# Layer 1 of a two-layer attention kernel: a block's values copied out in front of its softmax sums, one k addition moved behind two z additions, and the first two score copies exchanged between two engines

## The chip, the cores and the metric

The kernel runs on one core of one Trainium2 chip, as one program of about 131,000 instructions. The metric is the device time of one execution in microseconds, taken as the median of several runs. A profiled execution was recorded beside them. Its trace gives every instruction's start and duration on each engine: TensorE (PE for its matmuls, PEld for its weight loads), VectorE (DVE), ScalarE (ACT), GpSimd (POOL) and SyncE (SP, whose queue starts most of the transfers).

## The reference, cut to what matters

The input is x with 8 batch elements of 512 channels and 32 x 32 positions, in fp32. Layer 0 is a group norm, an attention of 8 heads and a projection, with a residual. The change touches layer 1 alone. For each batch element b, T = 1024 positions, 8 heads g of 64 channels:

```python
q, k, v = w_q @ xf, w_k @ xf, w_v @ xf           # xf = group_norm(x), per head 64 x 1024
attn = einsum('bhdq,bhdT->bhqT', q, k) * scale   # scores
attn = einsum('gh,bhqT->bgqT', w_head, attn)     # heads mixed
attn = softmax(attn, axis=-1)
attn = (attn - mean) / sqrt(var + EPS)           # over all (q, T) of a head
attn = attn * in_gamma + in_beta
out  = einsum('bhqT,bhdT->bhqd', attn, v)        # values
out  = out.reshape(b, t, c) @ w_proj.T + b_proj
x    = x + out
```

The kernel uses that the row sums of a softmax are 1, so that only the sum of squares has to be collected for the variance. It multiplies the exponentials with v first, and divides by the row sums later.

## The kernel before, in words

**Tiling.** Layer 1 takes the batch elements one after the other. The 1024 queries of an element are cut into NQB = 4 blocks of 256, the keys into 4 blocks of 256. One pair of blocks is done in two half-steps, so an element has NX = 32 of them, and a query block has QLAG = 8. The work is software-pipelined in `half_step(x)`, called with x = 0 to 36. It issues the scores of half-step x, the head mixing of half-step y = x - 4 (MLAG is 4) and the sums and values of half-step w = x - 5. No scheduler moves anything: each engine executes its instructions in the order in which the code issues them, and waits on semaphores for its operands and buffers.

**What a half-step issues.**
- `scores(x, i)` for i = 0, 1: 16 matmuls (L1656) into one PSUM tile of tag m, of which there are three buffers. It is then copied to SBUF into `raw`, on DVE (L1671) or on ACT (L1673). When both copies of an odd half-step are issued, eight transfers on SP's queue regroup `raw` into `re` (L1682), so that heads lie along partitions. Each is issued behind a particular matmul.
- `mix(y, j)` for j = 0, 1: 64 matmuls (L1706) with the head weights into another m tile, and ACT's exp from there to `e` (L1712).
- `squares(w, j)` on ACT (L1723), `sum_e` on DVE (a copy, L1728, in the first half-step of a block, then additions, L1730) and `sum_e2` on DVE (L1734). They collect the sums z and the sums of squares z2 over the eight half-steps of a block. In the first half-step of a block the squares are written into z2 directly.
- `values(w, i)` for i = 0, 1: 8 matmuls (L1752) into the accumulators a0 and a1, one PSUM bank each and with one buffer each. They run over the eight half-steps of a block, so the first values of the next block need both emptied.

TensorE's order within a half-step is: scores 0, mix 0, values 0, scores 1, mix 1, values 1.

**The end of a block.** `totals(qb)` is called when the last values of the block are issued. Its 16 matmuls with ones (L1783) sum z2 and then z over the partitions into an m tile. DVE copies one half of that into `row` (L1791), then ACT the other (L1792). Two transfers take `row` into the small tiles c0 and c1 (L1796), on POOL's queue for the blocks 0 to 2 and on SP's for the last. `leave(qb)` empties the accumulators into the attention output, which uses the q buffer: four copies of a1 on DVE (L1772) and four of a0 on ACT (L1774). For the inner blocks it is issued in the next half-step, behind its `scores(x, 0)`, and so behind the row copies. For the last block it is issued behind the whole loop, again behind the row copies. `reciprocals` (L1808, with a transfer to `zd`, L1810, and four broadcasts to `rzb`, L1814) and `divide` (L1842) follow, for the inner blocks 2 and 6 half-steps later.

**The end of an element.** During the last half-steps the k projection of the next element runs in pieces: seven products by TensorE (L1400), whose results DVE adds into sums and into k (L1415 to L1421, L1456). `k_leave()` issues the additions that are due, in each half-step between `sum_e` and `sum_e2`. The last of them, of product 3, is issued in half-step 36. Behind the loop come the last block's totals' consumers, part of the v projection (pv, L1475), a small matmul (pi, L1857) that gives the variance, the division, the affine pass (L1875, L1877), additions on DVE for the projection (L1375), and the output and q projections (pp and pq, L1400). The last element has no next one, and ends with `out1_last`, which interleaves the projection's products with these steps, and loads x again (xs_last, L1577).

**The start of an element.** The scores of half-step 0 need q, whose last parts DVE adds (L1512).

Of the kernel before, what the change touches and what calls it, by code (L numbers as in the profile page):

```python
# [467 lines left out]
def tile_two_attention_layers(  # L468
# [102 lines left out]
    NQB = 4  # L571
# [125 lines left out]
    with ExitStack() as l0:  # L697
# [486 lines left out]
        first = Agenda()  # L1184
# [80 lines left out]
    with ExitStack() as l1:  # L1265
# [14 lines left out]
        NX = 2 * NQB * NKB  # L1280
        QLAG = NX // NQB
        R_ORDER = (0, 4, 1, 5, 2, 6, 3, 7)
        MLAG = 4

        def m_psum(nm):
            return ps_m.tile([P, 2, FB], F32, tag="m", name=nm)
# [29 lines left out]
        def left_piece(key, i):  # L1316

            if i == 0:
                left_tile(key)
            f, r = i // 2, i % 2 * D  # L1320
            return nc.sync.dma_start(
                out=w_t[key][r : r + D, f],
                in_=left_d[key[0] + "1"][r : r + D, f * 2 * HC : (f + 1) * 2 * HC],
            )
# [26 lines left out]
        def y_piece(b, i):  # L1351

            if i == 0:
                y_t[b] = shared.tile([P, NCC, T], F32, tag="n", name=f"y_{b}")
            c, r = i // 4, i % 4 * 32
            return nc.sync.dma_start(
                out=y_t[b][r : r + 32, c], in_=x1_d[b][c * P + r : c * P + r + 32, :]
            )

        def normalize1(b, c):  # L1360
            normalize_to(y_t[b][:, c], b, c)
# [100 lines left out]
        def k_leave():  # L1462
            for fn in due:
                fn()
            due.clear()

        def v_pair(b, i):

            if i == 0:
                v_t[b] = shared.tile([P, NT, C], F32, tag="v", name=f"v1_{b}")  # L1470
            ps = m_psum(f"pv1_{b}_{i}")
            w = w_t["v", b]
            for m in range(2):
                for c in range(NCC):
                    nc.tensor.matmul(  # L1475
                        ps[:, m], y_t[b][:, c, ts(2 * i + m, P)], w[:, c],
                        start=(c == 0), stop=(c == NCC - 1),
                    )
            nc.scalar.copy(v_t[b][:, 2 * i], ps[:, 0])  # L1479
            nc.vector.tensor_copy(v_t[b][:, 2 * i + 1], ps[:, 1])  # L1480
# [158 lines left out]
        class Attention1:  # L1639
# [5 lines left out]
            def scores(self, x, i):  # L1645

                b, t, hp = self.b, x // 2, x % 2 * 2 + i
                qb, kb = t // NKB, t % NKB
                nm = f"s1_{b}_{x}_{i}"
                ps = m_psum(nm)  # L1650
                pv = ps.rearrange("p m (j k) -> p m j k", j=2)
                for j in range(2):
                    for c in range(2):
                        for m in range(2):
                            r = slice(m * D, m * D + D)
                            last = nc.tensor.matmul(  # L1656
                                pv[c * D : c * D + D, m, j],
                                qo_t[b][r, 2 * qb + j, hp, ts(c, D)],
                                k_t[b][r, hp, ts(kb, KB)], start=True, stop=True,
                            )  # L1660
                if x > MLAG:
                    self.piece(last)
                if x % 2 and i == 1:

                    order = (4, 5, 6, 7, 0, 1, 2, 3) if t == 1 else R_ORDER
                    self.due = [(t, r) for r in order]
                if x % 2 == 0 and i == 0:
                    self.raw[t] = rawpool.tile([P, H, 2, KB], F32, tag="raw", name=f"raw_{b}_{t}")
                dst = self.raw[t][:, 2 * hp : 2 * hp + 2]
                if i == 0 and (x < MLAG or x % 2):  # L1670
                    nc.vector.tensor_copy(dst, pv)  # L1671
                else:
                    nc.scalar.copy(dst, pv)  # L1673
# [204 lines left out]

            def half_step(self, x, ag):
                y, w = x - MLAG, x - MLAG - 1  # L1880
                first = 0 < w < NX and w % QLAG == 0
                if first:

                    self.scores(x, 0)
                    self.leave(w // QLAG - 1)
                if 0 <= w < NX:
                    self.squares(w, 0)
                    self.sum_e(w, 0)
                if x < NX and not first:
                    self.scores(x, 0)  # L1890
                if 0 <= w < NX:
                    self.squares(w, 1)
                    self.sum_e(w, 1)
                k_leave()
                if 0 <= w < NX:
                    self.sum_e2(w, 0)
                    self.sum_e2(w, 1)
                if 0 <= y < NX:
                    self.mix(y, 0)
                if 0 <= w < NX:  # L1900
                    self.values(w, 0)
                if x < NX:
                    self.scores(x, 1)
                if 0 <= y < NX:
                    self.mix(y, 1)
                ag.run(x - 0.75)
                if x <= MLAG or x >= NX:
                    self.regroup(n=NR)
                if x >= NX:
                    self.piece(n=len(self.pieces))  # L1910
                ag.run(x - 0.5)
                if 0 <= w < NX:
                    self.values(w, 1)
                    self.e.pop(w)
                    if w % QLAG == QLAG - 1:
                        qb = w // QLAG
                        self.totals(qb)
                        if qb < NQB - 1:
                            ag.at(x + 2, lambda: self.reciprocals(qb, ag, x + 2))
                            ag.at(x + 6, lambda: self.divide(qb))  # L1920
                ag.run(x)
# [5 lines left out]
        for b in range(B):  # L1927
            more = b + 1 < B
            a = Attention1(b)
            ag = Agenda()  # L1930

            for i, slot in enumerate((1, 3 - 0.75)):
                ag.at(slot, lambda i=i: v_pair(b, NV + i))
            if b == 0:
                for x, fn in enumerate(group_stages(B - 1, B, small_psum1)):
                    ag.at(x, fn)
                ag.at(3 - 0.75, v_sums)
            free = (NX // 2 - 2 + b) % 2
            if more:
                a.pieces += [lambda i=i: y_piece(b + 1, i) for i in range(4 * NCC)]  # L1940
                a.pieces += [lambda i=i: left_piece(("k", b + 1), i) for i in range(14)]
                for c in range(NCC):
                    ag.at(24 + c, lambda c=c: normalize1(b + 1, c))

                def k_begin():
                    kp.append(k_projection(b + 1))
                    kp[0].products(1)
                    kp[0].leave(1)

                def k_go(*ms):  # L1950
                    for m in ms:
                        kp[0].products(m)
                        due.append(lambda m=m: kp[0].leave(m))

                kp = []
                ag.at(NX - 0.5, lambda: right_tile(b + 1))
                ag.at(NX - 0.5, k_begin)
                ag.at(NX, lambda: right_y(b + 1, [0, 1]))
                ag.at(NX, lambda: k_go(2))
                ag.at(NX + 1, lambda: right_y(b + 1, [2, 3]))  # L1960
                ag.at(NX + 1, lambda: k_go(6, 7))
                ag.at(NX + 1, lambda: load_w(("v", b + 1), wvT, re_t[:, free, : NCC * C]))
                ag.at(NX + 1, lambda: left_p(b))
                ag.at(NX + 2, lambda: k_go(5, 4))
                ag.at(NX + 3, lambda: k_go(3))
            else:
                a.pieces += [lambda i=i: p_piece(i) for i in range(2 * NCC)]
            for x in range(NX + MLAG + 1):
                a.half_step(x, ag)

            a.leave(NQB - 1)
            if not more:
                ag.flush()
                out1_last(a)
                continue
            a.reciprocals(NQB - 1)
            a.instance()
            ag.flush()
            v_pair(b + 1, 0)
            a.instance_end()  # L1980
            a.divide(NQB - 1)
            for g in range(H):
                a.affine(g)
            right_o = re_t[:, 1 - free].rearrange("p (i k t) -> p i k t", i=4, k=2)
            combine_right(right_o, out_view(b))
            op = out1(b, right_o)
            load_left(("q", b + 1))
            v_pair(b + 1, 1)
            op.run()
            q_projection(b + 1).run()  # L1990
# [70 lines left out]
```

## Time and profile before

| | |
|---|---|
| time, median of 3 runs | 4268.98 us (4268.31 to 4270.03) |
| the profiled execution | 4269.45 us, of which its span 4267.5 us |
| layer 1 | from about 1812 us to the end |
| TensorE clock granted | 0.997 |
| one half-step of layer 1 in its steady part, two groups of scores, mix and values | about 5.94 us |
| VectorE, copy of a 128 x 1024 score tile from PSUM (L1671) | 1223 ns |
| ScalarE, the same (L1673) | 1015 ns |
| VectorE, one copy of 64 x 256 out of an accumulator (L1772) | median 422 ns, 128 of them |
| ScalarE, the same (L1774) | median 367 ns, 128 of them |
| VectorE, row copy (L1791), and ScalarE's (L1792) | 691 and 585 ns, 32 each |
| VectorE, addition of a 128 x 1024 tile (L1730, L1734) | 1218 and 1219 ns |

How to read it: the table's durations are those of single instructions. The lines that show what waits for what stand in the prediction. There, a line of the chain or of the timeline begins with its start and its duration in us, counted from the start of the span; a line of the waits has the total, how often it occurred, and the longest. An engine's name with the letter q means its queue or sequencer.

### The profile page before, as it was taken

What the parts mean: (1) busy time and instruction counts of PE and PEld (TensorE: products, weight loads), DVE (VectorE), ACT (ScalarE), POOL (GpSimd) and SP (SyncE); (2) the same over time, 40 slices, a digit from 0 to 9 for tenths busy, and PEclk for the clock granted to TensorE, in tenths of its full rate; (3) what the DMA queues carried; (4) which work ended last, traced back from release to release, by engine and by line L of the source; (5) the groups of instructions that cost most, each with busy time, mean ns of one, the idle gap of its engine ahead of it and who ended that gap; (6) DMA issues with size and microseconds to landing.
All of it is one profiled execution on the core that took longest, in us unless ns stands there. A gap on an engine that the chain in (4) does not pass through costs nothing.

```text
span 4267.5 us, 131379 instructions
## 1 busy us (share of the span) xinstructions
PE 4158.3 (97%) x58572; PEld 2213.3 (52%) x58572; DVE 2862.8 (67%) x3780; ACT 2319.2 (54%) x2735; POOL 53.3 (1%) x86
## 2 busy tenths in 40 slices
PE   7999999999999999999999999999999999999998
PEld 4353535353535353466466466466466466465565
DVE  4748484848484848558668668578578578587587
ACT  1717171727272726268268278187187286286385
POOL 0000000000000000000000000000000000000000
PEclk9999999999999999999999999999999999999999
DMA  4213131212121212167377287277386385485474
GB/s 148 78 49 109 47 110 45 86 45 85 45 85 45 84 47 83 56 169 192 111 180 190 93 199 186 99 197 185 96 202 166 103 205 155 121 204 142 136 179 136
DMA packets 253872, 521.99 MB, mean 122 GB/s; under 512 B 51889, under 2 KB 59441, under 8 KB 246641
## 3 DMA queue, kind: packets, MB, share of 16 engines
q1 hardware_dynamic: 248416, 510.71, 42.4%
q8 instruction: 461, 7.55, 0.7%
q0 software_dynamic: 2576, 0.69, 0.3%
q10 hardware_dynamic: 2304, 2.10, 0.2%
q14 instruction: 115, 0.93, 0.1%
HBM read 197.16 MB, written 46.92 MB: 57 GB/s over the span
## 4 chain that ended last, share of the span: by engine, by line
PE 90%; DVE 4%; ACT 2%; DMA 2%; issue 1%; SPq 0%; POOL 0%; DVEq 0%; ACTq 0%; POOLq 0%
PE a L1752 11%; PE s L1656 11%; PE m L1706 11%; PE s L1083 10%; PE a L1109 10%; PE pp_p L903 5%; PE pk_p L903 5%; PE pq_p L903 4%; PE pv_p L903 4%; PE pk L1400 4%; PE pq L1400 4%; PE pv L1475 4%; PE pp L1400 3%; PE t L1783 2%; ACT q L1774 1%
## 5 line engine op out<-in xcount | busy, mean ns | idle before, releaser
L1706 PEld LDWEIGHTS m<-wmix,re 64*64 64x64 f32 x32768 | 580.8, 135 | 117.1 <-issue 57.5
L1088 ACT ACTIVATE e<-s 128x1024 f32<-128x1024 f32 x512 | 497.2, 1026 | 234.2 <-PE s L1083 233.8
L1706 PE MATMUL m<-wmix,re 64*64 64x64 f32 x32768 | 591.0, 219 | 22.4 <-issue 19.7
L1712 ACT ACTIVATE e<-m 128x1024 f32<-128x1024 f32 x512 | 528.1, 1032 | 147.1 <-PE m L1706 142.6
L1752 PE MATMUL a<-e,v 128*64 128x256 f32 x4096 | 556.3, 392 | 25.0 <-ACT q L1774 20.9
L1730 DVE TENSOR_TENSOR z<-z,e 128x1024 f32<-128x1024 f32 x448 | 537.8, 1218 | 62.3 <-ACT e L1712 62.3
L1734 DVE TENSOR_TENSOR z<-z,e 128x1024 f32<-128x1024 f32 x448 | 534.2, 1219 | 44.4 <-ACT e L1723 43.7
L1656 PE MATMUL s<-k,q 64*64 64x256 f32 x8192 | 555.8, 389 | 5.8 <-DVE q L1512 2.6
L1096 DVE TENSOR_TENSOR zacc<-zacc,e 128x1024 f32<-128x1024 f32 x384 | 468.6, 1220 | 90.4 <-ACT e L1088 69.3
L1673 ACT COPY raw<-s 128x1024 f32<-128x1024 f32 x368 | 373.4, 1015 | 251.9 <-PE s L1656 229.6
L1083 PE MATMUL s<-q,k 64*64 64x512 f32 x4096 | 490.1, 593 | 2.3 <-ACT e L1088 2.3
L1109 PE MATMUL a<-e,v 64*64 64x512 f32 x4096 | 484.1, 589 | 0.0
L1723 ACT ACTIVATE e<-e 128x1024 f32<-128x1024 f32 x448 | 461.7, 1062 | 0.0
L1656 PEld LDWEIGHTS s<-k,q 64*64 64x64 f32 x8192 | 267.7, 132 | 272.9 <-issue 169.4
L1752 PEld LDWEIGHTS a<-e,v 128*64 128x64 f32 x4096 | 250.8, 136 | 147.1 <-ACT q L1774 24.2
L1109 PEld LDWEIGHTS a<-e,v 64*64 64x64 f32 x4096 | 156.7, 133 | 282.8 <-issue 282.8
L1083 PEld LDWEIGHTS s<-q,k 64*64 64x64 f32 x4096 | 147.9, 133 | 275.2 <-issue 241.4
L1671 DVE COPY raw<-s 128x1024 f32<-128x1024 f32 x144 | 176.0, 1223 | 102.5 <-PE s L1656 93.8
L1475 PE MATMUL pv<-re,y 128*128 128x512 f32 x480 | 214.5, 600 | 0.0
L1475 PEld LDWEIGHTS pv<-re,y 128*128 128x128 f32 x480 | 89.1, 191 | 113.3 <-issue 112.6
L903 PE MATMUL pv_p<-left_v,tmp 128*128 128x256 f32 x512 | 115.0, 383 | 4.2 <-DVE tmp L932 4.2
L1480 DVE COPY v<-pv 128x512 f32<-128x512 f32 x30 | 20.7, 689 | 139.6 <-ACT v L1479 139.6
(315 smaller groups left out, 4050.3 us busy)
## 6 DMA issues: line engine op xcount, KB each, us to landing
re<-raw SPq DMA_DIRECT2D x1024, 256.0 KB
rzb<-zd SPq DMA_DIRECT2D x256, 128.0 KB
left_q<-left_q SPq DMA_DIRECT2D x17, 1792.0 KB
left_p<-left_p SPq DMA_DIRECT2D x17, 1792.0 KB
left_k<-left_k SPq DMA_DIRECT2D x10, 1792.0 KB
x<-in_x_dram SPq DMA_DIRECT2D x32, 512.0 KB
x<-x SPq DMA_DIRECT2D x64, 256.0 KB
left_v<-left_v SPq DMA_DIRECT2D x8, 1792.0 KB
```

Of the source, the lines that this page charges most:

```text
L903: nc.tensor.matmul(out, st, mv, start=start, stop=(k == 1), skip_group_check=True)
L1083: nc.tensor.matmul(ps[c * D : c * D + D, m], k[r, hp, k0 : k0 + D], q[r, hp, ts(f, FB)], start=True, stop=True,)
L1088: nc.scalar.activation(e[i], ps, AF.Exp, scale=S0 * S0)
L1109: nc.tensor.matmul(acc[g][a][m * D : m * D + D], v[rows, kc, ts(2 * hp + m, D)], e[i][rows, m], start=(kc == 0), stop=(kc == NG - 1),)
L1400: nc.tensor.matmul(self.ps[m][:, i], w[:, left, k * HC + i * P : k * HC + i * P + P], right[:, k], start=(k == 0 and m != 2), stop=(k == 1 ...
L1475: nc.tensor.matmul(ps[:, m], y_t[b][:, c, ts(2 * i + m, P)], w[:, c], start=(c == 0), stop=(c == NCC - 1),)
L1656: last = nc.tensor.matmul(pv[c * D : c * D + D, m, j], qo_t[b][r, 2 * qb + j, hp, ts(c, D)], k_t[b][r, hp, ts(kb, KB)], start=True, stop=True,
L1706: last = nc.tensor.matmul(ps[c * D : c * D + D, a, ts(r, D)], self.re[t, r][rows, j, k0 : k0 + D], wmix[rows].rearrange("p g i -> p (g i)" ...
L1712: nc.scalar.activation(self.e[y][:, j], ps.rearrange("p a c -> p (a c)"), AF.Exp)
L1730: nc.vector.tensor_add(self.z[:, j], self.z[:, j], self.e[y][:, j])
L1734: nc.vector.tensor_add(self.z2[:, j], self.z2[:, j], self.e2[j])
L1752: last = nc.tensor.matmul(self.acc[w][two * D : two * D + D, s].rearrange("p (c i) -> p c i", i=Q8), v_t[b][:, kc, ts(g, D)], e[:, g], sta ...
```

## The change

It has three parts.

1. `leave(qb)` is issued in the half-step that issues the last values of the block, directly in front of `totals(qb)`. That holds for all four blocks, so the call behind the loop goes. On ACT and DVE the q copies then stand in front of the row copies. The special order of the first half-step of a block goes as well: `scores(x, 0)` stands behind the first `squares` and `sum_e`, as in every other half-step, so that DVE's copy of those scores stands behind the first of two z copies.
2. In half-step 36 the due addition of the k projection (L1456) is issued behind `sum_e2`, in front of which it stood. In the half-steps before that nothing changes: the second `k_leave()` finds nothing to do there.
3. The condition `i == (x == 0)` is true for i = 1 at x = 0, and for i = 0 otherwise. In half-step 0 of every element ACT copies the first score tile and DVE the second, where it was the other way round. All other half-steps keep their engines.

The order of TensorE's, POOL's and SP's instructions is the same in both kernels. DVE and ACT have the same instructions in another order.

```diff
-                if i == 0 and (x < MLAG or x % 2):
+                if i == (x == 0) and (x < MLAG or x % 2):
                     nc.vector.tensor_copy(dst, pv)
                 else:
                     nc.scalar.copy(dst, pv)
...
             def half_step(self, x, ag):
                 y, w = x - MLAG, x - MLAG - 1
-                first = 0 < w < NX and w % QLAG == 0
-                if first:
-
-                    self.scores(x, 0)
-                    self.leave(w // QLAG - 1)
                 if 0 <= w < NX:
                     self.squares(w, 0)
                     self.sum_e(w, 0)
-                if x < NX and not first:
+                if x < NX:
                     self.scores(x, 0)
                 if 0 <= w < NX:
                     self.squares(w, 1)
                     self.sum_e(w, 1)
-                k_leave()
+                if x < NX + MLAG:
+                    k_leave()
                 if 0 <= w < NX:
                     self.sum_e2(w, 0)
                     self.sum_e2(w, 1)
+                k_leave()
                 if 0 <= y < NX:
                     self.mix(y, 0)
...
                     if w % QLAG == QLAG - 1:
                         qb = w // QLAG
+                        self.leave(qb)
                         self.totals(qb)
...
             for x in range(NX + MLAG + 1):
                 a.half_step(x, ag)
-
-            a.leave(NQB - 1)
             if not more:
```

## The prediction

> **What bounds the kernel now.** I read the page's first part, then TensorE's waits (who waited for whom: total us, times, longest), then the chain of waits in two windows and the timeline at the end of a batch element.
>
> ```profile
> PE 4158.3 (97%) x58572; PEld 2213.3 (52%) x58572; DVE 2862.8 (67%) x3780; ACT 2319.2 (54%) x2735; POOL 53.3 (1%) x86
> ```
>
> TensorE (PE) is the bound: 4267.5 - 4158.3 = 109 us of the span is not matmul. The order of its instructions is the same in both kernels, so all that the change can move is in these 109 us. The waits show who owns them:
>
> ```profile
> PE a L1752 <- ACT q L1774: 20.9, 24, 0.9
> PE m L1706 <- issue: 19.7, 34, 2.1
> ...
> PE t L1783 <- DVE z L1734: 5.5, 8, 0.9
> ...
> PE s L1656 <- DVE q L1512: 2.6, 7, 0.4
> ...
> PE m L1706 <- DMA re<-raw: 2.2, 5, 0.7
> ```
>
> The first line is the same gap 24 times: 8 batch elements x 3 inner block boundaries. The chain of waits across one of them:
>
> ```profile
> 1900.39 1.01 PE a L1752 x8
> 1901.41 1.90 PE t L1783 x16
> 1903.33 0.70 DVE row L1791
> 1904.06 0.59 ACT row L1792
> 1904.64 0.26 ACT q L1774
> ...
> 1905.67 0.38 ACT q L1774
> 1906.09 1.08 PE a L1752 x8
> ```
>
> ACT's four q copies, which empty accumulator 0, stand behind ACT's row copy. That waits for DVE's row copy, and that for the column sums t. But accumulator 0 was complete at about 1898.5: its last a group is the one before the one shown. The next block's first values (a at 1906.09) need it empty.
>
> The timeline of all engines at an element's end:
>
> ```profile
> 2067.75 1.95 PE L1752 MATMUL a<-e,v 128*64 128x256 f32 x16
> ...
> 2067.86 1.22 DVE L1456 TENSOR_TENSOR k<-pk,sum 128x1024 f32<-128x1024 f32 x1 [2.08 <-PE pk L1400]
> ...
> 2069.00 2.35 DVE L1734 TENSOR_TENSOR z<-z,e 128x1024 f32<-128x1024 f32 x2
> ...
> 2070.36 2.95 PE L1783 MATMUL t<-z,ones 128*32 128x512 f32 x16 [0.66 <-DVE z L1734]
> ...
> 2073.24 7.13 PE L1475 MATMUL pv<-re,y 128*128 128x512 f32 x16
> ```
>
> The sums t wait for the two additions L1734, which stand behind the k addition L1456. t starts 0.66 us late and takes 2.95 us instead of 1.90, as its third matmul group waits for the second addition.
>
> [...] ACT sat 2.57 us before the row copy at 1904.06 with the q copies ready behind it. [...] the rows have 422 and 367 ns, which I use.
>
> **Part A, leave in front of totals at 24 inner boundaries.** No instruction is added; four q copies on ACT (1.50 us) and four on DVE (1.72 us) change places with the row copies. DVE's scores copy also moves, behind the first of the two z copies.
>
> What goes. From one a group to the next takes 1903.19 - 1901.34 = 1.85 us of t, plus an ordinary half of a half-step, 2.97 us (starts 1894.39, 1897.36), so 4.82 us; it took 1906.09 - 1900.33 = 5.76. The stall is 0.94 us, and the same 5.76 is at the last element's third boundary (4179.24 to 4185.00). The PE wait row gives 0.87 each, the weight loads' row (24.2 us in 24) 1.01. I take 0.94 x 24 = 22.6 us, bounds 20.9 and 24.2.
>
> What is late next. ACT is free at 1901.48 (exp at 1900.46 + 1.02), so its q copies end at 1903.0, before values want the accumulator at 1905.1. On DVE the q copies wait for the last a group (1901.41) and run 1901.5 to 1903.25; t ends at 1903.3, so the row copy starts as before. If they slip, the row slips as much; the next user of t's buffer is the scores group at 1906.1, and ACT's row copy ends at 1904.65: 1.4 us of margin. DVE goes on: z copy to 1904.65, scores copy to 1905.9, where it ended at 1905.6. Its PSUM buffer is wanted by the second mix at 1907.0: 1.1 us of margin. ACT's squares still start behind the row copy, now with no q copies between, so the next exp comes at 1906.7 instead of 1908.09. The sums' DMAs on POOL's queue start from the same ACT row end. The regroup DMAs on SP's queue are issued behind the same matmuls, about 1 us earlier.
>
> **Part B, the end of an element.** The k addition moves behind the two L1734 additions on DVE, in 7 elements (the last has no next k). The additions then start when the squares and DVE allow: L1730 ends at 2065.77, so they run to 2068.1, before the values end at 2069.7. So t starts at 2069.75 and takes 1.85: end 2071.6, where pv started at 2073.24. That is 1.64 us x 7 = 11.5 us; the rows at elements 2 to 6 show the same 0.66 and 2.95. The k addition then ends at 2069.35; its PSUM buffer is next used by the small matmul pi at 2080, its k tile by the next element's scores, at 2136. DVE's q copies follow, 2069.8 to 2071.5, and the row copy starts at 2071.7 instead of 2073.36. So the row's DMA, the reciprocal, the broadcast, the division and the affine pass, which hold the pp matmuls at 2087.5, all come some 1.65 us earlier too, which they must: the second pv group ends at 2087.46, so pp has no slack. Bounds of B: 11.8 us (0.66 + 1.03 each), and 0 if that chain does not follow. At the last element nothing waits behind k; t stays late, and the q copies fit before the row copy (DVE free at 4225.75, + 1.72 = 4227.5, row at 4227.76). There the chain ends:
>
> ```profile
> 4232.18 0.25 DVE rz L1808
> 4232.43 0.03 DVE junk L1826
> 4232.46 6.32 DMA zd<-rz
> ```
>
> The reciprocal can come 0.75 us earlier, since q copies no longer stand between row and the wsum additions. But its little transfer takes 6.32 us here, against 1.75 at the first element, behind the four 512 KB xs_last loads, whose issue on SP ends at 4232.25; it can be issued only 0.2 us earlier. I count 0.1 us, bounds 0 and 0.75.
>
> **Part C, the first score copies.** At half-step 0 the copy of the first four-matrix group goes to ACT, that of the second to DVE. ACT is idle 14.5 us there, DVE adds q until 2138.44; the buffer is free at 2138.4 instead of 2139.58. But PE's next user starts 1.07 us after the group before it, where 1.03 is ordinary: 0.04 x 7 = 0.3 us, bounds 0 and 0.4. The DVE copy ends at 2139.68 and pv wants that buffer at 2140.66.
>
> **Sum.** 22.6 + 11.5 + 0.1 + 0.3 = 34.5 us. The profiled execution took 4269.45 (span 4267.5, 1.95 around it), so 4234.95; it stands 0.47 above the median of 4268.98, so 4234.5.
>
> **Rivals.**
> 1. Transfers take up the gain. The issue row (19.7 us, irregular) and the waits on re<-raw stand in stretches where the DMA engines are 0.79 to 0.86 busy (1900 to 1930 and 1925 to 1955). Without the stall PE asks for the same bytes in about 2% less time. Against: only five waits on re<-raw, 2.2 us in all. If half of A went there: 4268.98 - 11.3 - 11.9 = 4245.8.
> 2. B buys nothing: pv starts earlier, but pp waits for the division, because the broadcast lands late or DVE's q copies hold up the row. For: no slack before pp. Against: each link starts from the row. 4268.98 - 23.0 = 4246.0.
> 3. Slower: the scores copy behind q, row and z holds its PSUM buffer. Place: the second mix after each boundary. It decides from a copy end at 1907.0, 1.1 us after what I work out, and outweighs A and B from a stall of 34.5/24 = 1.44 us. With 2 us the time is 4268.98 - 34.5 + 24 x 2.0 = 4282.5. Against: everything in front of it on DVE is ready.
> 4. The order of the instructions moves, but the wait stays (accumulator 0 released by something later than the q copies, k kept ahead): about 4268. Against: in the built order the values wait for ACT alone, and k stands behind both additions.
>
> **How the numbers follow.** Forecast 0.78; rival 1 0.08; rival 2 0.08; rival 3 0.03; rival 4 0.03. The forecast's own range is 4229 (A at 24.2, and 3 us less of issue gaps) to 4241 (A at 20.9, B at 10, and 3 us more); up to 4246 takes in rivals 1 and 2. A measurement of this kernel can tell 0.2% (8.5 us) from no change: faster 0.94, same 0.03, slower 0.03.
>
> **What would show it.** A: the row "a waits for ACT q" gone, 4.82 us between the a groups around t, the row copies not later. B: no wait of t at L1734 but the last element's, t in 1.9 us, no new wait at the first pp. C: nothing that can be seen. A new wait of m on DVE's scores copy, or issue gaps far above 20 us, would make it wrong.

## The result, and the profile after

| | before | changed |
|---|---|---|
| time, median | 4269.5 us (4268.31 to 4270.77, 4 runs) | 4233.14 us (4225.8 to 4242.1, 4 runs) |
| ratio to before, 95% interval | | 0.9914 (0.9901 to 0.9926) |
| the profiled execution | 4269.45 us, span 4267.5 | 4225.8 us, span 4223.7 |

The change makes the kernel 36.4 us faster; 4234.5 was forecast. The profiled execution of the changed kernel was the fastest of its four, so the two traces differ by more than the medians, by 43.65 us.

The page's first part, changed kernel (engine, busy us, share of the span, instructions):

```profile
PE 4147.2 (98%) x58572; PEld 2212.8 (52%) x58572; DVE 2861.1 (68%) x3780; ACT 2317.5 (55%) x2735; POOL 60.3 (1%) x86
```

The engines have the same instructions. TensorE's share is 98% now, since 4223.7 - 4147.2 = 76.5 us of the span is not matmul, against 109. The span is 43.8 us shorter, so 11.1 us of that came out of TensorE's busy time.

TensorE's waits in the changed kernel (line and tile that waited, releaser: total us, times, longest):

```profile
PE m L1706 <- issue: 12.0, 22, 1.4
PE m L1706 <- DMA re<-raw: 4.5, 10, 0.7
...
PE s L1656 <- DVE q L1512: 2.6, 7, 0.4
...
PE pp L1400 <- DVE re L1375: 1.6, 7, 0.2
...
PE t L1783 <- DVE z L1734: 1.0, 1, 1.0
```

The row of 24 waits of a on ACT's q copies is gone. Of t's eight waits on the z additions one is left, the last element's. No row of m on DVE's scores copy has come, and pp waits for the same additions as before, 0.2 us each.

The timeline of the three engines across the boundary whose chain the prediction shows, changed kernel (start, duration in us, engine, line, operation; in brackets the idle time ahead and its releaser):

```profile
1899.26 1.08 PE L1752 MATMUL a<-e,v 128*64 128x256 f32 x8
...
1900.27 1.92 PE L1783 MATMUL t<-z,ones 128*32 128x512 f32 x16
1900.31 1.49 ACT L1774 COPY q<-a 64x256 f32<-64x256 f32 x4
1900.39 1.73 DVE L1772 COPY q<-a 64x256 f32<-64x256 f32 x4 [1.67 <-PE a L1752]
...
1902.26 0.69 DVE L1791 COPY row<-t 128x512 f32<-128x512 f32 x1
1902.87 0.68 DVE L1728 COPY z<-e 128x1024 f32<-128x1024 f32 x1
...
1903.47 1.22 DVE L1671 COPY raw<-s 128x1024 f32<-128x1024 f32 x1
...
1904.08 1.08 PE L1752 MATMUL a<-e,v 128*64 128x256 f32 x8
...
1906.01 1.11 PE L1706 MATMUL m<-wmix,re 64*64 64x64 f32 x64
```

From a to a it is 1904.08 - 1899.26 = 4.82 us, against 5.76. Both engines' q copies now run while TensorE sums t. They end at 1901.80 on ACT and 1902.12 on DVE, and the row copy starts 1.99 us after t started, as it did before (1903.33 - 1901.34). The scores copy ends at 1904.69, and the mix that reuses its buffer starts at 1906.01: 1.3 us to spare.

The timeline at an element's end, changed kernel:

```profile
2061.22 2.35 DVE L1734 TENSOR_TENSOR z<-z,e 128x1024 f32<-128x1024 f32 x2
2063.28 1.95 PE L1752 MATMUL a<-e,v 128*64 128x256 f32 x16
2063.49 1.22 DVE L1456 TENSOR_TENSOR k<-pk,sum 128x1024 f32<-128x1024 f32 x1
...
2065.16 1.92 PE L1783 MATMUL t<-z,ones 128*32 128x512 f32 x16
2065.28 1.73 DVE L1772 COPY q<-a 64x256 f32<-64x256 f32 x4 [0.56 <-PE a L1752]
2067.01 7.13 PE L1475 MATMUL pv<-re,y 128*128 128x512 f32 x16
2067.15 0.69 DVE L1791 COPY row<-t 128x512 f32<-128x512 f32 x1
...
2081.29 1.98 PE L1400 MATMUL pp<-q,left_p 128*128 128x512 f32 x4
```

The two z additions end at 2063.57, before the values do, and the k addition comes behind them. From the values to pv it is 2067.01 - 2063.28 = 3.73 us, against 2073.24 - 2067.75 = 5.49. From pv to pp it is 14.28 us, against 14.27: the whole chain from the row copy to the projection moved with pv, so the gain stays.

Set side by side, the two traces give this:

| | removed, us |
|---|---|
| 24 inner boundaries, 0.94 each | 22.6 |
| 7 element ends, values to pv, 5.49 to 3.73 | 12.3 |
| 7 element starts, the scores just ahead of pv, start to pv, 2.07 to 1.89 | 1.3 |
| last element, start of its t to the end of the span, 42.74 to 41.63 | 1.1 |
| irregular gaps: m, s and a on "issue", 22.6 to 13.5, and m on re<-raw, 2.2 to 4.5 | 6.8 |
| sum, of 43.65 | 44.1 |

The row of irregular gaps is the part that no edit explains. The profiled execution happened to have fewer such gaps; the experiments say more on it.

### The profile page after: what moved, and what is told of

Its sections match the earlier page's. It is cut to its first block, busy times and chain, and to the rows that moved or that the text cites. A ratio compares the mean times of both kernels' runs of the same rounds, so it can differ in the third digit from the quotient of the medians.

```text
span 4223.7 us, 131372 instructions
## 1 busy us (share of the span) xinstructions
PE 4147.2 (98%) x58572; PEld 2212.8 (52%) x58572; DVE 2861.1 (68%) x3780; ACT 2317.5 (55%) x2735; POOL 60.3 (1%) x86
## 2 busy tenths in 40 slices
DMA packets 253871, 521.99 MB, mean 124 GB/s; under 512 B 51888, under 2 KB 59440, under 8 KB 246640
## 3 DMA queue, kind: packets, MB, share of 16 engines
q8 instruction: 461, 7.55, 0.7%
## 4 chain that ended last, share of the span: by engine, by line
PE 92%; DVE 4%; DMA 2%; ACT 1%; issue 1%; SPq 0%; POOL 0%; DVEq 0%; ACTq 0%; POOLq 0%
PE a L1752 12%; PE s L1656 11%; PE m L1706 11%; PE s L1083 11%; PE a L1109 10%; PE pp_p L903 5%; PE pk_p L903 5%; PE pq_p L903 4%; PE pv_p L903 4%; PE pk L1400 4%; PE pq L1400 4%; PE pv L1475 4%; PE pp L1400 3%; PE t L1783 1%; DMA re<-raw 1%
```

## The experiments

Each kernel was timed beside the kernel before on the same chip. The medians of before in the three batches were 4273.97, 4277.14 and 4275.0 us, some 5 to 8 us above the 4268.98 shown first, so ratios and differences within a batch are what counts. The gains given below are the ratios' own; differences of the medians come out up to 2.6 us larger (22.7, 14.8, 0.8 and 35.0 us for e1 to e4), inside the intervals. Theory: each part takes away its own wait and nothing comes in its place. Rivals: transfers or a new wait take part of the gain back.

### The three parts alone

`e1_leave_alone` has part 1 of the change only, with the k addition and the first score copies as before:

```diff
 # against the changed kernel
-                if i == (x == 0) and (x < MLAG or x % 2):
+                if i == 0 and (x < MLAG or x % 2):
...
-                if x < NX + MLAG:
-                    k_leave()
+                k_leave()
...
-                k_leave()
```

> The kernel before with part A alone (q copies in front of totals, scores copy behind the first z copy; k addition and first score copies as before). Theory: the 24 waits of values for ACT's q copies go, 0.94 us each: 22.6 us faster, about 4247 us against 4269.5, ratio 0.9947. t still waits for L1734 in 8 places (5.5 us), with 2.95 us per t at an element's end. Rival (transfers take up part of A): 11 us faster, waits on re<-raw and issue gaps grow by as much. Rival (scores copy holds its PSUM buffer): a new wait of m on DVE raw, and not faster.

Measured: 4251.32 us (4249.71 to 4255.6), ratio 0.9951 (0.9938 to 0.9965). TensorE's waits of this run:

```profile
PE m L1706 <- issue: 17.3, 37, 1.2
PE t L1783 <- DVE z L1734: 6.3, 8, 1.7
...
PE m L1706 <- DMA re<-raw: 2.8, 8, 1.0
```

The 24 waits of a are gone and t's eight stay. Waits on transfers are 2.8 us in place of 2.2, and all issue gaps 22.1 in place of 22.6: they did not take the 20 us.

`e2_k_alone` has part 2 only:

```diff
 # against before
-                k_leave()
+                if x < NX + MLAG:
+                    k_leave()
                 if 0 <= w < NX:
                     self.sum_e2(w, 0)
                     self.sum_e2(w, 1)
+                k_leave()
```

> The kernel before with part B alone (last k addition behind the last two z2 additions). Theory: t starts 0.66 us earlier and takes 1.9 us at seven element ends, and the chain to pp follows: 11.5 us faster, about 4258 us, ratio 0.9973. The 24 waits for ACT's q copies stay at 20.9 us. Rival (pp's chain does not follow): not faster, a new wait of pp on the q or re additions of about 1.6 us in 7 places.

Measured: 4259.18 us (4257.09 to 4264.43), ratio 0.997 (0.9958 to 0.9981): 12.8 us by the ratio, with an interval of 8 to 18. The 24 waits of a are all there, and of t's eight only one is left:

```profile
PE a L1752 <- ACT q L1774: 20.8, 24, 0.9
...
PE t L1783 <- DVE z L1734: 0.9, 1, 0.9
```

`e3_score_copies_alone` has part 3 only:

```diff
 # against before
-                if i == 0 and (x < MLAG or x % 2):
+                if i == (x == 0) and (x < MLAG or x % 2):
```

> The kernel before with part C alone (engines of the two first score copies exchanged). Theory: 0.3 us faster, not to be told from no change, ratio 1.000. Rival: the copy on DVE comes later than ACT's did and delays the first pv by its PSUM buffer: up to 0.5 us slower in 7 places, 3.5 us.

Measured: 4273.16 us (4266.98 to 4284.12), ratio 1.0 (0.9992 to 1.0009), and both waits are there (from the scores just ahead of pv to pv it is 1.89 us in this trace, against 2.07 before):

```profile
PE a L1752 <- ACT q L1774: 20.9, 24, 0.9
...
PE t L1783 <- DVE z L1734: 6.6, 8, 1.9
```

`e4_changed_again` is the changed kernel, unedited, beside these three.

> The changed kernel once more, five times, for its scatter: the four runs so far lie between 4225.8 and 4242.1 us, those of the kernel before between 4268.3 and 4270.8. If the scatter belongs to the kernel, the runs spread over 10 us or more again, around 4233. If it was chance of one chip, they lie within 3 us. A profile differs from the earlier one in TensorE's issue gaps and waits on re<-raw alone (together 18.4 us there).

Measured: 4239.0 us (4233.95 to 4242.33), ratio 0.9923 (0.991 to 0.9937). The parts alone sum to 20.9 + 12.8 + 0 = 33.7 us, by their ratios; the whole gives 32.9. They are additive within what can be measured. Its profiled run had 16.3 us of issue gaps ahead of m and 2.5 us of waits on re<-raw, together 18.8 us against the first one's 12.0 + 4.5 = 16.5. Runs of the kernel before spread over 11.6 us in this batch as well (4267.95 to 4279.53, 19 runs). So the scatter isn't something that the change brought.

### Which half of part 1 does it

`leave` was cut in two, so that one engine's q copies stand in front of the row copies and the other's behind:

```diff
-                        self.leave(qb)
+                        self.leave(qb, (0,))
                         self.totals(qb)
+                        self.leave(qb, (1,))
```

That is `e5_act_half_early` (ACT's copies in front, DVE's behind); `e6_dve_half_early` has 0 and 1 exchanged. `leave(qb, ws)` loops over `ws` instead of both accumulators.

> The changed kernel, but of leave only ACT's copies of accumulator 0 stand in front of totals; DVE's of accumulator 1 stand behind the row copy again. Theory: the wait of the next block's values for ACT q is gone as in the changed kernel. But DVE now has row, q, z copy, scores copy in this order, so the scores copy ends about 1907.55 on the scale of the first boundary, where the second mix wants its buffer at 1907.0: a new wait of m on DVE raw of 0.55 to 0.6 us in 24 places, 14 us slower than the changed kernel, about 21 us faster than the kernel before (ratio 0.995). Rival (DVE's copies have slack enough, the place of the scores copy does not matter): as fast as the changed kernel, ratio 0.992, no wait of m on raw.

Measured: 4254.75 us (4253.66 to 4259.87), ratio 0.995 (0.9936 to 0.9963), half of part 1's gain lost again. Its waits, and then its timeline behind a boundary:

```profile
PE m L1706 <- DVE raw L1671: 10.5, 24, 0.4
```

```profile
1904.04 0.69 DVE L1791 COPY row<-t 128x512 f32<-128x512 f32 x1 [3.54 <-PE t L1783]
1904.65 1.72 DVE L1772 COPY q<-a 64x256 f32<-64x256 f32 x4
...
1906.40 0.70 DVE L1728 COPY z<-e 128x1024 f32<-128x1024 f32 x1
...
1907.13 1.23 DVE L1671 COPY raw<-s 128x1024 f32<-128x1024 f32 x1
...
1908.41 1.16 PE L1706 MATMUL m<-wmix,re 64*64 64x64 f32 x64 [0.44 <-DVE raw L1671]
```

DVE does nothing for 3.54 us ahead of the row copy, though the accumulator that its q copies read was complete at 1902.12 (the a group at 1901.04 took 1.08 us), and then has the q copies, a z copy and the scores copy in a row. The scores copy ends at 1908.36, and the mix that needs its buffer starts at 1908.41 instead of 1907.79 (the a group at 1905.86 plus the 1.93 us from there to the mix in the changed kernel): 0.62 us, of which the wait view counts 0.44. This is rival 3's mechanism, brought on by moving 1.72 us of DVE work to the wrong side of the row copy, against a margin of 1.3 us.

> The changed kernel, but of leave only DVE's copies of accumulator 1 stand in front of totals; ACT's of accumulator 0 stand behind ACT's row copy again. Theory: all of A's gain hangs on ACT's copies: the wait of a on ACT q is back with 0.87 us in 24 places, and only B and C stay: 12 us faster than the kernel before, ratio 0.997. Rival (the row copy itself, or t, holds the values): the wait is shorter or gone.

Measured: 4261.54 us (4260.09 to 4268.68), ratio 0.9967 (0.9956 to 0.9979), which is what part 2 alone gives. The wait of a is back at its full length:

```profile
PE a L1752 <- ACT q L1774: 21.0, 24, 0.9
```

So ACT's copies behind the row copy are the cause of the old stall. DVE's have to move with them only because, in the changed kernel's order, the scores copy stands behind them and would be late. The other way out, DVE's order left as it was (row, scores copy, q copies) with ACT's copies alone in front, was not tried.

`e7_scores_first` is the changed kernel with the first scores of a block in their old place, ahead of the first z copy on DVE:

```diff
+                first = 0 < w < NX and w % QLAG == 0
+                if first:
+                    self.scores(x, 0)
...
-                if x < NX:
+                if x < NX and not first:
                     self.scores(x, 0)
```

> The changed kernel with the old order of the first scores of a block (scores in front of the first squares and sum_e, so that DVE's scores copy stands in front of both z copies). Theory: the scores copy has 1.1 us of margin either way; as fast as the changed kernel, ratio 0.992. Rival (the copy behind a z copy costs something): 24 x 0.3 us = 7 us faster than the changed kernel, ratio 0.990.

Measured: 4243.12 us (4240.04 to 4246.91), ratio 0.9923 (0.991 to 0.9937), the same as e4's, and no wait of m on the scores copy. The place ahead of the z copy brings the scores copy forward by 0.2 us only (it starts 3.01 us after t in place of 3.20, since it then waits for its scores, which in the changed kernel's profile end 2.94 us after t starts), and that buys nothing once the copy is on time.

### Do transfers take up the gain, and what are the issue gaps?

`e8_more_transfers` is the changed kernel with a useless transfer of 256 KB from DRAM to DRAM behind each piece of streamed weights and activations, 282 in all. The moved bytes go from 521.99 to 595.94 MB; nothing that is computed changes.

```diff
+                        spare = dram.tile(
+                            [D, T], F32, tag=f"spare_{next(spares)}", name="spare"
+                        )
+                        extra = nc.sync.dma_start(out=spare, in_=x1_d[self.b][0:D])
+                        behind(extra, ins)
```

> The changed kernel with one extra transfer of 256 KB from one place of device memory to another behind each of the pieces that are loaded during the first 20 or so half-steps of an element (its result is used by nothing). For the gaps of TensorE that no wait explains (issue) and the waits on re<-raw, together 18 to 22 us in the changed kernel. Theory: the issue gaps are TensorE's instructions arriving late, on the same DMA engines: they grow to 30 us or more and lie where the extra transfers run, at one position modulo 128 matmuls. Rival (they are late re<-raw transfers or unrecorded matmuls): the waits on re<-raw grow instead, or nothing grows.

Measured: 4329.03 us (4320.49 to 4334.94), ratio 1.0119 (1.0104 to 1.0135), 86 us above e7 on the same chip. Its waits (its lines are shifted by up to 7):

```profile
PE m L1713 <- DMA re<-raw: 49.7, 71, 2.2
PE m L1713 <- issue: 25.7, 42, 1.4
```

Waits on the regrouped scores grew about tenfold. Issue gaps, counted over all of layer 1, came to 31.2 us in 51, against 13 to 21 in runs of the changed kernel. So both the theory's and its rival's signs came. Against e7's profile the span is 88.1 us longer: 45.3 us are waits on re<-raw and 9.3 us issue gaps. Another 29.1 us are counted as busy time of TensorE (4181.8 against 4152.7), most of it in the mixing matmuls; whether these are waits hidden in the records is not shown. So with 14% more bytes waits on transfers are real and heavy; at the bytes that the kernel has, the rows show a few microseconds. The extra transfers went through SP's queue, among the regroup transfers, so this run does not tell the load on the DMA engines from the place in the queue.

The issue gaps have a pattern. TensorE's timeline of this run, a stretch with three of them:

```profile
3766.01 1.09 PE L1713 MATMUL m<-wmix,re 64*64 64x64 f32 x58 [0.64 <-issue]
3767.03 1.08 PE L1759 MATMUL a<-e,v 128*64 128x256 f32 x8
3768.04 1.09 PE L1658 MATMUL s<-k,q 64*64 64x256 f32 x16
3768.95 0.87 PE L1713 MATMUL m<-wmix,re 64*64 64x64 f32 x46
3771.12 0.50 PE L1713 MATMUL m<-wmix,re 64*64 64x64 f32 x18 [1.30 <-issue]
3771.56 1.08 PE L1759 MATMUL a<-e,v 128*64 128x256 f32 x8
...
3779.43 0.75 PE L1713 MATMUL m<-wmix,re 64*64 64x64 f32 x38
3780.50 0.67 PE L1713 MATMUL m<-wmix,re 64*64 64x64 f32 x26 [0.32 <-issue]
```

From the first gap to the second it is 58 + 8 + 16 + 46 = 128 matmuls. From the second to the third it is 18 + 8 + 16 + 64 + 8 + 16 + 64 + 8 + 16 + 38 = 256 (the seven groups left out are s, and then m, a and s twice). The page counts 58572 weight loads beside 58572 matmuls, so 128 matmuls are 256 instructions. The page's list of queues has one of kind "instruction" (q8) with 461 packets and 7.55 MB:

```profile
q1 hardware_dynamic: 257440, 584.65, 45.2%
q8 instruction: 461, 7.55, 0.7%
```

That is 16.4 KB each. TensorE has 117,499 recorded instructions, the 355 of its sequencer included: 459 stretches of 256, against 461 packets. The two counts fit together: at an issue gap TensorE seems to be waiting for its next packet of instructions.

The recorded packets bear this out. Number TensorE's recorded instructions in order. Then all 485 issue gaps ahead of layer 1's groups in the 13 profiles lie at number 193 or 194 modulo 256, and none elsewhere. When a gap ahead of number 256 n + 193 (or 194) ends, exactly n packets of q8 have landed, in all 485, and packet n landed 1.1 to 1.7 us before (1.23 to 1.60 us in the 38 gaps of the kernel before, 1.27 to 1.64 in the 25 of the changed kernel's first profile). And of the 372 blocks of 256 that begin there in layer 1 of each of these two profiles, none began less than 1.23 us after its packet had landed. By these records the gaps are waits for instruction packets that landed late. Why some came late is less sure: e8 has 51 late ones in place of 25 to 35, but no experiment moved these packets alone. The waits on re<-raw stand at no such position.

`e9_spread_pieces` tried to win some of these gaps back. The pieces of weights and activations that stream in during the first part of an element are issued one with each group of scores there; here at half that rate, and the rest later:

```diff
-                if x > MLAG:
+                if x > MLAG and (i == 1 or x % 8 < 2 or x > 24):
```

> The changed kernel with the pieces of y and of the k weights (30 transfers of 128 KB in an element) loaded at half the rate in the first half of an element, and the rest in its second half; the broadcasts of rzb keep their rate. If the issue gaps and the waits on re<-raw come from the load on the DMA engines there, they fall from 18 to 26 us to about 12 us, and the kernel is 5 to 12 us faster than the changed one (ratio 0.990 or lower against 0.9923). Rival (the gaps belong to the program, whatever the load): they stay, and so does the time.

Measured: 4238.36 us (4235.95 to 4243.62), ratio 0.992 (0.9907 to 0.9934), with 17.6 us of issue gaps in 33 and 6.8 us of waits on re<-raw in 16. The gain did not come.

`e10_spread_z_first` adds to that the sums of z in front of those of z2 in `totals`, so that t's first half does not wait for the last additions, which are those of z2:

```diff
-                for m, z in ((1, self.z2), (0, self.z)):
+                for m, z in ((0, self.z), (1, self.z2)):
```

> As the run before, and in totals the sums of z come in front of those of z2. Theory: the only wait of t that is left, at the last element, where the z2 additions come last on DVE, covers half of t's matmuls then: t ends about 1.4 us earlier there, which no timing can show, but the trace can (t starts right behind the values; its longest wait falls from 1.9 us). Otherwise as the run before.

Measured: 4238.41 us (4235.04 to 4241.57), ratio 0.9916 (0.9902 to 0.9929). `e11_changed_third` is the changed kernel once more, beside these two.

> The changed kernel beside the two runs before on the same chip, so that they can be compared: ratio 0.992 to the kernel before.

Measured: 4238.65 us (4236.83 to 4247.39), ratio 0.9921 (0.9907 to 0.9935). The last t in the trace of e10, and then in that of e11:

```profile
4196.92 2.71 PE L1783 MATMUL t<-z,ones 128*32 128x512 f32 x16
```

```profile
4195.78 2.95 PE L1783 MATMUL t<-z,ones 128*32 128x512 f32 x16 [1.39 <-DVE z L1734]
```

The wait ahead of t went as meant. A shorter one stayed inside t, which took 2.71 us where t takes 1.92 without a wait. From the start of the last values to the end of t it is 5.80 us in e10 and 7.51 in e11, a difference that the scatter of the times hides. None of these versions measurably beats the changed kernel.

## Why the prediction was right

**Part 1: right in place and size.** The step said 24 stalls of 0.94 us, 22.6 in all. The stall went, from a to a it took the 4.82 us worked out, and alone it was timed at 20.9 us, with an interval of 15 to 26. The reason given, that ACT's q copies stood behind a row copy for which they had no need to wait, is shown by e5 and e6: moving ACT's copies removes the wait, moving DVE's does not. That DVE's had to move too, in this order, was in the step as a margin of 1.1 us for the scores copy. The trace has 1.3, and e5, which overruns it, stalls at exactly the named mix. One statement ahead of the step was wrong, without harm to the sum: that all the change can move is in the 109 us in which TensorE is not busy. Of the 43.8 us by which the span fell, 11.1 were busy time, 7.2 of them in t (69.8 to 62.6 us), whose records had covered part of its wait. The sum was safe since it was worked out from starts.

**Part 2: right, a little small.** 1.64 us x 7 = 11.5 was forecast. The trace has 1.76 x 7 = 12.3, and alone it was timed at 12.8 (8 to 18). The step let t start 2.0 us behind the start of the values, at their recorded end. It starts 1.88 behind, since the recorded ends of matmuls overlap with the next ones (the values' last end is recorded at 2065.23, t's start at 2065.16), and the 0.12 us is the difference. The bound of 0, that the chain to pp would not follow, did not come in: pv to pp is 14.28 us against 14.27.

**Part 3: nothing that can be timed, as said.** e3's ratio is 1.0. The term was mis-sized: 0.04 us per element start was forecast, and the traces have 0.18 (scores to pv 2.07 to 1.89). Seven of these are 1.3 us, about a sixth of the width of e3's interval (7.3 us). That they belong to part 3 is shown by e3's own trace, which has the 1.89 too.

**The last element: a small term, mis-sized.** 0.1 us was forecast, with a bound of 0.75. From t to the end it took 41.63 us in the first profile of the changed kernel and 42.42 in e11, against 42.74: 1.1 and 0.3. The reciprocal did come 1.18 us earlier (6.24 us after t's start against 7.42). But the issue of zd came only 0.12 us earlier (7.58 against 7.70), since SP was still issuing xs_last (until 4189.56 in the first changed profile, with zd issued at 4189.65); the prediction had 0.2 for that. Most of what remains is how long the two transfers behind it took. From zd's issue to rzb's it was 5.99 and 6.70 us in the two changed runs, against 6.33, and from rzb's issue to the division 4.63 and 4.55, against 5.10. With the 0.12 us (0.11 in e11) that makes 0.93 of the 1.1, and 0.29 of the 0.3. The prediction took both transfers to last as before.

**The rivals.** Rival 1 (transfers take the gain): waits on re<-raw were 2.2 us before and 2.5, 4.5 and 5.0 in three profiles of the changed kernel, so at most some 3 us more, and the row of issue gaps ahead of m was 12.0 to 18.4 against 19.7. e8 shows that transfers can hold TensorE up, at 74 MB more. Rival 2 fell with pv to pp, rival 4 with the waits. Rival 3 did not come; e5 shows its mechanism at work from the point where the margin is used up.

**The range.** It held, but not for all of the reasons given: 3 us were put down for issue gaps. Four runs of the changed kernel spread over 16 us and 19 of before over 11.6, so that the first median came within 1.4 us of the forecast is in part luck. The same kernel's profile in e11 is 14.5 us longer than the first: 7.5 us of that are issue gaps and waits on re<-raw (25.5 against 18.0) and 4.7 us TensorE's busy time. On the other two chips the ratios (0.9923 and 0.9921) put the gain at 33 to 34 us, and the medians at 35.0 and 36.4. Both are close to the sum of 34.5.

## What to carry to other kernels

When a stall recurs once per loop round on the busiest engine, follow the chain of waits back until an instruction is found that waits only because of what stands ahead of it in its queue. Moving that one is worth the stall's length times its count, provided that every instruction it then pushes back still ends before its reader wants it; write that margin down for each engine, as half of the move (e5) can cost half of the gain. Then ask whether the chain behind the stall starts from the moved point: only then does the gain last to the end.

## What the runs showed of the hardware

- TensorE has gaps that the trace calls issue: 13 to 21 us of layer 1 in 25 to 35 gaps of the changed kernel, and 31.2 us in 51 with 14% more bytes moved. All 485 in 13 profiles lie at one place in every 256 of its instructions, and end 1.1 to 1.7 us after a 16 KB instruction packet landed (461 packets, 7.55 MB): by these records they are waits for late instructions.
- Busy time of TensorE can cover waits: t's 16 matmuls took 2.95 us with a wait among them and 1.92 without, and of the span that the change saved, 11.1 us of 43.8 were counted as busy before.
- Extra transfers that grow the moved bytes by 14% cost about 2% here (4329 against 4243 us), with waits on regrouped scores of 49.7 us in place of 2.5 to 5, although the extra bytes are needed by nobody. They stood in the same queue as the regroup transfers, and load and queue order were not told apart.
- The times of one kernel on one chip spread over 8 to 17 us (e4 and e3), in a program on one core at a granted clock of 0.997 to 0.999 in these runs.
